# Re-ordering the last mixture-of-experts stage: first expert chunk behind the closing chunks, two smaller scan parts, gates in three groups, all read-backs at once

## The chip, the cores and the metric

The kernel runs on one core of a Trainium2 chip. The metric is device time in microseconds from the first to the last instruction of that core; lower is better. The engines are PE (matrix multiply), PEld (its weight loads), DVE (VectorE), ACT (ScalarE), POOL (GpSimd, which here issues all indirect gathers and scatters) and SP (which issues the plain DMAs).

## The reference, cut to what matters

The model has two layers, each a graph part plus a token mixer followed by a mixture of experts. The change touches only the last mixture of experts, `_L1_ffn_ref`, whose router is itself a small graph attention over 32768 edges between the first 2048 rows (B = 16, N = 128 in the source shapes; here it is called with one batch of 3125 rows):

```python
h = (x_flat @ W_gat).reshape(M, HEADS, NUM_EXPERTS)          # 4 heads, 4 experts
a_src = (h * att_src).sum(-1); a_dst = (h * att_dst).sum(-1)
e = leaky_relu(a_src[src] + a_dst[dst], 0.2)                  # per edge, loops added
alpha = exp(e - segment_max(e, dst)[dst]) / segment_sum(...)
agg = segment_sum(h[src] * alpha, dst) + b_gat
scores = layernorm(agg).reshape(M, HEADS, NUM_EXPERTS).mean(1)
topk_s, topk_i = top_k(scores, 2); w = softmax(topk_s)
for ei in range(4):
    g = where(topk_i == ei, w, 0).sum(-1)
    out = out + g * (gelu(x @ W1[ei] + b1[ei]) @ W2[ei] + b2[ei])
```

The expert outputs are computed for every row, the gates are needed only at the end: the matrix products of the experts and the per-edge work of the router can run side by side.

## The kernel before

The 3125 rows are 25 tiles of 125 rows (`P = 125`, `NT = 25`), grouped in seven chunks, `CHUNKS` (L22): four of 4 tiles and three of 3 tiles. The last stage is `layer1_ffn` (L1654). It goes through these steps.

**Closing chunks.** `close_graph` (L1906) finishes the layer before and feeds this stage. It runs a three-deep pipeline over chunks, steps c = 0 to 8: `in_units(c + 2)` scales on ACT, `moments(c)` adds to `x` and takes mean and variance on DVE, `rows(c - 1)` normalises on DVE, transposes on PE (L1951) and copies to `xT` on ACT (L1952), and `scores(c - 2)` multiplies by the router's weights on PE (L191), copies the result to `srow` and `row` on ACT (L1960, L1961) and stores `srow` to the table `tabg` in HBM. A dictionary `beside` names a step behind which a function is called; before, step `len(CHUNKS) - 3`, that is c = 4, calls the first expert's first chunk, `expert(0, *CHUNKS[0], *w)`. PE, DVE and ACT take all of this in the order in which it is written (`manual_schedule`, L1726).

**Scatters.** POOL scatters the 25 tiles of `row` to the table `starts` (line 58 as seen by the trace), tile by tile as `row` becomes ready.

**Gathers.** Each of the 256 edge columns (`EC = 256`, 128 edges each) needs one indirect gather of `tabg` rows into the tile `G` (`sources`, L1686; line 51 in the trace). They wait for all of `tabg`.

**Experts.** `expert` (L1704) runs 4 experts over 7 chunks: hidden products on PE into `fph` (L1709), GELU on ACT (L1711), second product on PE into `fpy` (L1717), bias add on DVE (L1719). Experts 0 and 1 stay in SBUF (`y`, `acc`), experts 2 and 3 are stored to HBM (`yd`). In this loop only DVE is held to the written order (L1801).

**Scans.** `scan(f0, f1)` (L1772) turns edge columns f0 to f1 into running segment sums: DVE adds and a running maximum (L1777 to L1784), two exponentials on ACT (L1786, L1792), a product (L1789) and 20 running sums (L1796), then a DMA of those columns of `G` to `sums` in HBM (L1797). `parts` (L1800) says behind which expert chunk (counted 1 to 28) which columns are scanned: the last part, columns 194 to 255, comes behind chunk 28.

**Carry and gates.** A short chain (L1820 to L1856) makes the carry between partitions, `taken`. POOL then gathers `g_r`, one row of `sums` per tile, 25 gathers. The outputs of experts 2 and 3 are loaded back as `yback`, four chunks at once and the others as one of five buffers is free (L1862 on). `graph_gates` (L1977) computes the gates for a group of tiles: DVE arithmetic, two exponentials, a square root (L2033), `top_two` (L625) in blocks of 5 tiles, another exponential, a normalisation. Two groups are used, chunks 0 to 3 (16 tiles) and chunks 4 to 6 (9 tiles).

**Totals.** For each tile the four expert outputs times their gates are added to `x`: even tiles of a chunk by four DVE instructions (L1892), odd tiles by four diagonal matrices from ACT (L1900), five PE products (L1898, L1902) and an ACT copy (L1903). A chunk is then stored to the output.

In this last part no engine is held to the written order; the program's planner may move instructions of one group between those of another.

Of the kernel before, what the change touches and what calls it, by code (L numbers as in the profile page):

```python
# [18 lines left out]
D = 256  # L19
P = 125  # L20
NT = 25
CHUNKS = ((0, 4), (4, 4), (8, 4), (12, 4), (16, 3), (19, 3), (22, 3))  # L22
# [20 lines left out]
E2, EC = 32768, 256  # L43
# [31 lines left out]
def rows_of(table):  # L75
    return table.rearrange("(t p) d -> p t d", p=P)
# [12 lines left out]
class Kernel:  # L89
# [532 lines left out]
                                     pattern=[[1, ne], [-1, ne]], channel_multiplier=0)  # L622
        return tie

    def top_two(self, pool, v, ne, tag, tie):  # L625

        nc, n = self.nc, v.shape[1]
        mask = pool.tile([P, n, ne], F32, name="mask" + tag)
        rank = pool.tile([P, n, ne], F32, name="rank" + tag)
        for t0 in range(0, n, 5):  # L630
            m = min(5, n - t0)
            s = slice(t0, t0 + m)
            shape = [P, m, ne, ne]
            gt = pool.tile([P, 5, ne, ne], F32, name="gt" + tag)[:, :m]
            eq = pool.tile([P, 5, ne, ne], F32, name="eq" + tag)[:, :m]
# [1018 lines left out]
    def layer1_ffn(self):  # L1654
        nc, tc, a = self.nc, self.tc, self.a
        NE, FC = 4, 4
        R = 24
        C = 25
        with ExitStack() as c:
            big = c.enter_context(tc.tile_pool(name="f1", bufs=1))  # L1660
            ps_a = c.enter_context(tc.tile_pool(name="f1pa", bufs=2, space=PSUM))
            ps_h = c.enter_context(tc.tile_pool(name="f1ph", bufs=3, space=PSUM))
# [41 lines left out]
            def expert(ei, t0, n, w1, w2, b2):  # L1704
                hs = wk.tile([128, FC, 4 * P], F32, name="fh")
                for f in range(FC):
                    ph = ps_h.tile([128, 4 * P], F32, name="fph")
                    for k in range(2):
                        nc.tensor.matmul(ph[:, :n * P], w1[:, k, f * 128:(f + 1) * 128],  # L1709
                                         xT[:, k, t0 * P:(t0 + n) * P], start=(k == 0), stop=(k == 1))  # L1710
                    nc.scalar.activation(hs[:, f, :n * P], ph[:, :n * P], AF.Gelu,  # L1711
                                         bias=self.col("L1_ffn_b1", ei * FC + f))
                out = y[ei][:, t0:t0 + n, :] if ei < 2 else wk.tile([P, 4, D], F32, name="fy")
                for i in range(n):
                    py = ps_y.tile([P, D], F32, name="fpy")
                    for f in range(FC):
                        nc.tensor.matmul(py, hs[:, f, i * P:(i + 1) * P], w2[:, f, :],  # L1717
                                         start=(f == 0), stop=(f == FC - 1))
                    nc.vector.tensor_add(out[:, i, :], py, b2)  # L1719
                if ei >= 2:  # L1720
                    move(nc.sync, rows_of(yd[ei - 2])[:, t0:t0 + n, :], out[:, :n, :])

            E_ = mybir.EngineType
            w = weights(0)
            with tc.tile_pool(name="f1l", bufs=1, side="right") as lp, \
                    tc.manual_schedule(engines={E_.PE, E_.DVE, E_.Activation}):  # L1726
                nc.vector.memset(row, 1.0)
                self.close_graph(lp, ps_a, ps_y, xT, acc, den, srow, row, tabg,
                                 beside={len(CHUNKS) - 3: lambda: expert(0, *CHUNKS[0], *w)})

                nc.vector.tensor_add(loop, srow[:, :, 16:20], row[:, :, 0:4])
                nc.vector.scalar_tensor_tensor(loop, loop, 0.2, loop, op0=OP.mult, op1=OP.max)
# [64 lines left out]
                nc.sync.dma_start(sums[:].rearrange("(p f) c -> p f c", p=128)[:, s, :], G[:, s, :])  # L1797


            parts = {10: (0, 80), 16: (80, 138), 22: (138, 194), 28: (194, EC)}  # L1800
            with tc.manual_schedule(engines={mybir.EngineType.DVE}):  # L1801
                step = -(-EC // (NE * len(CHUNKS)))
                sources(3 * step)
# [58 lines left out]
            rs = ga.tile([P, NT, R], F32, name="g_r", bufs=1)  # L1862
            backs = []
            for t0, n in CHUNKS:
                back = ga.tile([P, 2, 4, D], F32, name="yback", bufs=5)
                for i in range(2):
                    move(nc.sync, back[:, i, :n, :], rows_of(yd[i])[:, t0:t0 + n, :])
                backs.append(back)
                if len(backs) == 4:
                    break  # L1870
            for t in range(NT):
                gather(nc, rs[:, t, :], sums[:], self.seg_at[:, 1, t:t + 1])
            for c0, c1 in ((0, 4), (4, 7)):
                ta, tb = CHUNKS[c0][0], CHUNKS[c1 - 1][0] + CHUNKS[c1 - 1][1]
                more = ps_a.tile([P, 16, C], F32, name="ln_pt")
                for t in range(ta, tb):
                    nc.tensor.matmul(more[:, t - ta, :], ends[:, t * P:(t + 1) * P], taken, start=True, stop=True)
                gate = self.graph_gates(ga, ta, tb, rs, more[:, :tb - ta, :], loop, srow, vec, tie)
                for k in range(c0, c1):
                    t0, n = CHUNKS[k]  # L1880
                    if k < len(backs):
                        back = backs[k]
                    else:
                        back = ga.tile([P, 2, 4, D], F32, name="yback", bufs=5)
                        for i in range(2):
                            move(nc.sync, back[:, i, :n, :], rows_of(yd[i])[:, t0:t0 + n, :])
                    for t in range(t0, t0 + n):
                        outs = [y[ei][:, t, :] if ei < 2 else back[:, ei - 2, t - t0, :] for ei in range(NE)]
                        xs = self.x[:, t, :]
                        if (t - t0) % 2 == 0:  # L1890
                            for ei in range(NE):
                                nc.vector.scalar_tensor_tensor(xs, outs[ei], gate[:, t - ta, ei:ei + 1], xs,  # L1892
                                                               op0=OP.mult, op1=OP.add)
                            continue

                        diag = ga.tile([P, NE, P], F32, name="diag", bufs=3)
                        pm = ps_h.tile([128, 4 * P], F32, name="fph")[:P, :D]
                        nc.tensor.matmul(pm, self.ident[:P, :P], xs, start=True, stop=False)  # L1898
                        for ei in range(NE):
                            nc.scalar.activation(diag[:, ei, :], self.ident[:P, :P], AF.Copy,  # L1900
                                                 scale=gate[:, t - ta, ei:ei + 1])
                            nc.tensor.matmul(pm, diag[:, ei, :], outs[ei], start=False, stop=(ei == NE - 1))  # L1902
                        nc.scalar.copy(xs, pm)  # L1903
                    move(nc.sync, rows_of(self.out)[:, t0:t0 + n, :], self.x[:, t0:t0 + n, :])

    def close_graph(self, pool, psum, psum_g, xT, acc, den, srow, row, tabg, beside):  # L1906

# [69 lines left out]
    def graph_gates(self, ga, ta, tb, rs, more, loop, srow, vec, tie):  # L1977


        nc = self.nc  # L1980
        NE, n, s = 4, tb - ta, slice(ta, tb)
        r, loop = rs[:, s, :], loop[:, s, :]
# [15 lines left out]
        nc.vector.tensor_scalar(c2[:, :, 0, :], c2[:, :, 0, :], 0.0, None, op0=OP.min)  # L1998
        nc.vector.tensor_sub(c2[:, :, 1, :], loop, m)
        nc.scalar.activation(c2, c2, AF.Exp)  # L2000
        nc.vector.tensor_mul(c2[:, :, 0, :], c2[:, :, 0, :], hasb)
        agg = ga.tile([P, n, 16], F32, name="agg", bufs=1)
        own = ga.tile([P, n, 16], F32, name="g_own", bufs=1)
# [27 lines left out]
        nc.vector.tensor_mul(sq, agg, agg)  # L2031
        nc.vector.tensor_reduce(mu, sq, AX.X, OP.add)
        nc.scalar.activation(mu, mu, AF.Sqrt, bias=self.eps[:P], scale=1.0 / 16)  # L2033
        nc.vector.reciprocal(mu, mu)
        nc.vector.tensor_mul(agg, agg, mu[:, :, None].to_broadcast([P, n, 16]))
        nc.vector.tensor_mul(agg, agg, all_tiles(vec["ln_gamma"]))
# [1 line left out]
        sc = ga.tile([P, n, NE], F32, name="s_sc", bufs=1)  # L2038
        nc.vector.tensor_reduce(sc, agg.rearrange("p t (h e) -> p t e h", h=4), AX.X, OP.add)
        nc.vector.tensor_scalar(sc, sc, 0.25, None, op0=OP.mult)  # L2040
        mask = self.top_two(ga, sc, NE, "s", tie)
        gate = self.softmax_parts(ga, sc, NE, "s")
        nc.vector.tensor_mul(gate, gate, mask)
        self.normalise(ga, gate, NE, "s")
        return gate


@with_exitstack
# [42 lines left out]
```

## Time and profile before

| | us |
|---|---|
| runs (median of 3; lowest to highest) | 3070.16 (3053.29 to 3075.47) |
| the profiled execution, whole | 2708.31 |
| its span, first to last instruction | 2706.6 |
| PE busy | 2183.3 (81%) |
| POOL busy | 1661.2 (61%) |
| DVE busy | 1494.8 (55%) |
| ACT busy | 561.0 (21%) |

The profiled execution is 361.85 us shorter than the median of the runs; nothing in the profile says why. Times below are microseconds from the start of its span. In the last stage the following stretches can be told apart:

| stretch | us from the start | what runs |
|---|---|---|
| closing chunks with the first expert chunk among them | 2190 to 2254 | DVE, PE, ACT; POOL scatters from 2210.93 |
| expert loop | 2254 to 2592 | PE; POOL gathers `G` 2264.43 to 2595.5 |
| last scan and carry | 2597 to 2613 | DVE |
| gathers of `g_r` | 2614.93 to 2654.6 | POOL; loads of `yback` |
| gates and totals | 2641.6 to 2706.6 | DVE, ACT, PE |

A line of the timeline gives the start, the duration, the engine, the source line, the operation, output and input, the number of instructions that were merged, and in brackets the idle time of that engine just before and what ended it.

### The profile page before, as it was taken

Reading aid. Unit: us, or ns where it says so; the run is one execution under the profiler, and the core shown is the slowest. Engines: PE = TensorE matmul, PEld = TensorE weight load, DVE = VectorE, ACT = ScalarE, POOL = GpSimd, SP = SyncE. Lnnn points to the kernel's source line nnn. Section 1 sums busy time; section 2 is a strip of 40 time slices with the busy share of each in tenths; the row PEclk is TensorE's granted clock in tenths of the full one; section 3 lists DMA queues with packets and bytes.
Section 4 is the critical chain, followed back from the end, with each engine's and each line's share of the span. In section 5 each row is a group of like instructions: output and inputs, shape, how many; then the busy total and the mean of one; then the engine's idle time right before and its main releaser. Section 6 shows DMA issues by size and latency. Waiting matters only on the chain. (4 is left out here: it accounts for less than half of the span.)

```text
span 2706.6 us, 26634 instructions
## 1 busy us (share of the span) xinstructions
PE 2183.3 (81%) x9047; PEld 1643.4 (61%) x9047; DVE 1494.8 (55%) x3520; ACT 561.0 (21%) x1180; POOL 1661.2 (61%) x1486
## 2 busy tenths in 40 slices
PE   1852459999985999799999759999877779989953
PEld 1541347866754566588888646666655557666643
DVE  7977399465477931122122268998877762222226
ACT  1421000000001211122222244444100043132213
POOL 4888787776000731666666437778877726777751
PEclk9956669999995999899999879999899769999966
DMA  8930524043400212454555451111111121112252
GB/s 298 383 126 14 120 70 117 4 114 93 117 25 9 65 45 71 143 197 170 194 197 176 121 144 47 49 48 46 47 48 49 49 66 17 26 48 53 55 106 73
DMA packets 176141, 259.81 MB, mean 96 GB/s; under 512 B 54041, under 2 KB 141059, under 8 KB 172604
## 3 DMA queue, kind: packets, MB, share of 16 engines
q1 hardware_dynamic: 117803, 201.64, 24.0%
q0 software_dynamic: 52288, 47.17, 7.5%
q10 hardware_dynamic: 5894, 9.09, 1.0%
q8 instruction: 76, 1.25, 0.2%
q14 instruction: 80, 0.66, 0.1%
HBM read 173.99 MB, written 83.69 MB: 95 GB/s over the span
## 5 line engine op out<-in xcount | busy, mean ns | idle before, releaser
L58 POOL DMA_INDIRECT adj<-ch_sum,ch_place x391 | 508.3, 1300 | 149.9 <-issue 113.1
L51 POOL DMA_INDIRECT g<-tab,t_src x391 | 457.1, 1169 | 119.4 <-issue 108.7
L58 POOL DMA_INDIRECT sorted<-s_rows,pos x256 | 245.1, 958 | 182.0 <-DVE s_rows L1059 112.5
L460 PE MATMUL psum<-sup,adjT 125*125 125x256 f32 x1250 | 292.3, 393 | 52.7 <-DMA adjT<-adj 42.5
L1293 PE MATMUL pw<-v,hot 128*125 128x260 f32 x1244 | 306.9, 407 | 0.0
L51 POOL DMA_INDIRECT G<-tabg,g_src x256 | 253.4, 990 | 78.0 <-issue 71.3
L460 PEld LDWEIGHTS psum<-sup,adjT 125*125 125x125 f32 x1250 | 240.7, 194 | 94.1 <-DMA adjT<-adj 34.6
L1293 PEld LDWEIGHTS pw<-v,hot 128*125 128x125 f32 x1244 | 244.5, 200 | 43.6
L866 PE MATMUL ph<-xs,w 128*128 128x256 f32 x960 | 220.4, 389 | 23.6 <-issue 20.8
L866 PEld LDWEIGHTS ph<-xs,w 128*128 128x128 f32 x960 | 184.2, 194 | 59.0 <-issue 33.9
L894 PE MATMUL py<-w,h 128*128 128x256 f32 x960 | 216.7, 379 | 0.0
L894 PEld LDWEIGHTS py<-w,h 128*128 128x128 f32 x960 | 180.1, 190 | 23.3
L1717 PE MATMUL fpy<-fw,fh 128*125 128x256 f32 x800 | 181.4, 383 | 14.4 <-ACT fh L1711 11.7
L868 ACT ACTIVATE h<-ph,b 128x256 f32<-128x256 f32 x240 | 113.7, 474 | 363.0 <-PE ph L866 331.3
L1717 PEld LDWEIGHTS fpy<-fw,fh 128*125 128x125 f32 x800 | 150.3, 189 | 50.0 <-ACT fh L1711 15.0
L1709 PE MATMUL fph<-xT,fw 128*128 128x500 f32 (+1 forms) x448 | 177.2, 545 | 0.0
L1034 PE MATMUL pctx<-s_mv,s_ro 128*128 128x256 f32 x512 | 155.2, 414 | 1.9 <-DVE s_mv L1033 1.9
L58 POOL DMA_INDIRECT slots<-rows,abi x50 | 74.2, 1484 | 100.0 <-DVE r_cum L948 85.1
L897 DVE TENSOR_SCALAR yo<-py,own 128x256 f32<-128x256 f32 x60 | 27.8, 480 | 192.2 <-PE py L894 192.2
L463 DVE TENSOR_TENSOR x<-x,psum 125x512 f32<-125x512 f32 (+1 forms) x104 | 68.7, 663 | 108.8 <-PE psum L460 108.6
L1709 PEld LDWEIGHTS fph<-xT,fw 128*128 128x128 f32 x448 | 85.2, 192 | 71.4 <-issue 48.8
L170 ACT ACTIVATE ln_rs<-ln_mv,eps 125x4 f32<-125x4 f32 (+1 forms) x14 | 3.7, 294 | 586.6 <-DVE ln_mv L169 586.6
(550 smaller groups left out, 3423.9 us busy)
## 6 DMA issues: line engine op xcount, KB each, us to landing
adjT<-adj SPq DMA_DIRECT2D x25, 1367.2 KB
adj<-zero SPq DMA_DIRECT2D x22, 1536.0 KB
w<-in_L_ffn_W1p_dram SPq DMA_DIRECT2D x30, 1024.0 KB
w<-in_L_ffn_W2p_dram SPq DMA_DIRECT2D x30, 1024.0 KB
slots<-empty SPq DMA_DIRECT2D x1, 8448.0 KB
srow<-slots SPq DMA_DIRECT2D x30, 264.0 KB
adj<-ch_sum,ch_place POOLq DMA_INDIRECT x391
g<-tab,t_src POOLq DMA_INDIRECT x391
```

The costliest lines, as they stand in the source:

```text
L51: nc.gpsimd.indirect_dma_start(out=out, out_offset=None, in_=table, in_offset=bass.IndirectOffsetOnAxis(ap=idx, axis=0))
L58: return nc.gpsimd.indirect_dma_start(out=table, out_offset=bass.IndirectOffsetOnAxis(ap=idx, axis=0), in_=rows, in_offset=None, **kw)
L460: nc.tensor.matmul(pm[:, i, :], mats[b][:, (a0 + i) * P:(a0 + i + 1) * P], sup[:, b, :], start=(b == b0), stop=(b == b0 + n - 1))
L463: nc.vector.tensor_add(xs, xs, pm[:, :m, :])
L866: nc.tensor.matmul(ph, w1[:, k, f * 128:(f + 1) * 128], xs[:, k, :], start=(k == 0), stop=(k == 1))
L868: nc.scalar.activation(h[:, f, :], ph, AF.Gelu, bias=b1[:, f:f + 1])
L894: nc.tensor.matmul(py, h[:, f, i * 128:(i + 1) * 128], w2[:, f, :], start=(f == 0), stop=(f == FC - 1))
L897: nc.vector.tensor_scalar(yo, py, own[:, i, 2:3], None, op0=OP.mult)
L1034: nc.tensor.matmul(p1, ro[:, f - f0, :], mv, **st)
L1293: nc.tensor.matmul(pw.rearrange("p h c -> p (h c)"), hot[:, i - i0, :], v[:, i, :, :].rearrange("p h c -> p (h c)"), start=(i == i0), stop ...
L1709: nc.tensor.matmul(ph[:, :n * P], w1[:, k, f * 128:(f + 1) * 128], xT[:, k, t0 * P:(t0 + n) * P], start=(k == 0), stop=(k == 1))
L1717: nc.tensor.matmul(py, hs[:, f, i * P:(i + 1) * P], w2[:, f, :], start=(f == 0), stop=(f == FC - 1))
```

## The change

Five edits, all in the last stage.

- The first expert's first chunk is called behind step `len(CHUNKS) + 1`, the last step of the closing pipeline, and no longer behind c = 4.
- The last scan part (194 to 255) becomes two, 194 to 231 behind chunk 25 and 232 to 255 behind chunk 27, so that the last part stands before chunk 28 in DVE's order.
- All seven chunks of `yback` have a buffer of their own and are loaded before the gates.
- The gates are computed for three groups (chunks 0 and 1, 2 and 3, 4 to 6). `graph_gates` becomes a generator with three stops before it hands over the gate; at the first two stops of a group the totals of one waiting chunk of the group before are written in between. `top_two` takes blocks of 9 tiles there, and the softmax exponential is written ahead of it.
- PE, DVE and ACT are held to the written order in this part too.

```diff
-    def top_two(self, pool, v, ne, tag, tie):
+    def top_two(self, pool, v, ne, tag, tie, by=5):
...
-        for t0 in range(0, n, 5):
-            m = min(5, n - t0)
+        for t0 in range(0, n, by):
+            m = min(by, n - t0)
...
-                                 beside={len(CHUNKS) - 3: lambda: expert(0, *CHUNKS[0], *w)})
+                                 beside={len(CHUNKS) + 1: lambda: expert(0, *CHUNKS[0], *w)})
...
-            parts = {10: (0, 80), 16: (80, 138), 22: (138, 194), 28: (194, EC)}
+            parts = {10: (0, 80), 16: (80, 138), 22: (138, 194), 25: (194, 232), 27: (232, EC)}
...
-                back = ga.tile([P, 2, 4, D], F32, name="yback", bufs=5)
+                back = ga.tile([P, 2, 4, D], F32, name="yback", bufs=len(CHUNKS))
...
-                if len(backs) == 4:
-                    break
...
-            for c0, c1 in ((0, 4), (4, 7)):
+            def gates(c0, c1):
                 ta, tb = CHUNKS[c0][0], CHUNKS[c1 - 1][0] + CHUNKS[c1 - 1][1]
                 more = ps_a.tile([P, 16, C], F32, name="ln_pt")
                 for t in range(ta, tb):
                     nc.tensor.matmul(more[:, t - ta, :], ends[:, t * P:(t + 1) * P], taken, start=True, stop=True)
-                gate = self.graph_gates(ga, ta, tb, rs, more[:, :tb - ta, :], loop, srow, vec, tie)
+                for gate in self.graph_gates(ga, ta, tb, rs, more[:, :tb - ta, :], loop, srow, vec, tie):
+                    yield gate, ta
+            def total(k, gate, ta):
...
+            with tc.manual_schedule(engines={E_.PE, E_.DVE, E_.Activation}):
+                ready = []
+                for c0, c1 in ((0, 2), (2, 4), (4, 7)):
+                    for gate in gates(c0, c1):
+                        if gate[0] is None and ready:
+                            total(*ready.pop(0))
+                    while ready:
+                        total(*ready.pop(0))
+                    ready = [(k, *gate) for k in range(c0, c1)]
+                for r in ready:
+                    total(*r)
...
         nc.scalar.activation(c2, c2, AF.Exp)
+        yield None
         nc.vector.tensor_mul(c2[:, :, 0, :], c2[:, :, 0, :], hasb)
...
         nc.scalar.activation(mu, mu, AF.Sqrt, bias=self.eps[:P], scale=1.0 / 16)
+        yield None
...
-        mask = self.top_two(ga, sc, NE, "s", tie)
         gate = self.softmax_parts(ga, sc, NE, "s")
+        yield None
+        mask = self.top_two(ga, sc, NE, "s", tie, 9)
...
-        return gate
+        yield gate
```

`total` holds the lines of the loop over a chunk's tiles (L1887 to L1905) unchanged, and reads `backs[k]`.

More of the change, by code (lines that the diff above doesn't have):

```diff
@@ L629, in top_two @@
         rank = pool.tile([P, n, ne], F32, name="rank" + tag)
-        for t0 in range(0, n, 5):
-            m = min(5, n - t0)
+        for t0 in range(0, n, by):
+            m = min(by, n - t0)
             s = slice(t0, t0 + m)
             shape = [P, m, ne, ne]
-            gt = pool.tile([P, 5, ne, ne], F32, name="gt" + tag)[:, :m]
-            eq = pool.tile([P, 5, ne, ne], F32, name="eq" + tag)[:, :m]
+            gt = pool.tile([P, by, ne, ne], F32, name="gt" + tag)[:, :m]
+            eq = pool.tile([P, by, ne, ne], F32, name="eq" + tag)[:, :m]
             other = v[:, s, None, :].to_broadcast(shape)
@@ L1877, in layer1_ffn @@
                     nc.tensor.matmul(more[:, t - ta, :], ends[:, t * P:(t + 1) * P], taken, start=True, stop=True)
-                gate = self.graph_gates(ga, ta, tb, rs, more[:, :tb - ta, :], loop, srow, vec, tie)
[L1879 to L1898, printed above, removed]
-                        for ei in range(NE):
[L1900 to L1904, printed above, removed]
@@ new lines, in gates @@
+                for gate in self.graph_gates(ga, ta, tb, rs, more[:, :tb - ta, :], loop, srow, vec, tie):
+                    yield gate, ta
+            def total(k, gate, ta):
+                t0, n = CHUNKS[k]
+                for t in range(t0, t0 + n):
+                    outs = [y[ei][:, t, :] if ei < 2 else backs[k][:, ei - 2, t - t0, :] for ei in range(NE)]
+                    xs = self.x[:, t, :]
+                    if (t - t0) % 2 == 0:
+                        for ei in range(NE):
+                            nc.vector.scalar_tensor_tensor(xs, outs[ei], gate[:, t - ta, ei:ei + 1], xs,
+                                                           op0=OP.mult, op1=OP.add)
+                        continue
+                    diag = ga.tile([P, NE, P], F32, name="diag", bufs=3)
+                    pm = ps_h.tile([128, 4 * P], F32, name="fph")[:P, :D]
+                    nc.tensor.matmul(pm, self.ident[:P, :P], xs, start=True, stop=False)
+                    for ei in range(NE):
+                        nc.scalar.activation(diag[:, ei, :], self.ident[:P, :P], AF.Copy,
+                                             scale=gate[:, t - ta, ei:ei + 1])
+                        nc.tensor.matmul(pm, diag[:, ei, :], outs[ei], start=False, stop=(ei == NE - 1))
+                    nc.scalar.copy(xs, pm)
+                move(nc.sync, rows_of(self.out)[:, t0:t0 + n, :], self.x[:, t0:t0 + n, :])
```

## The prediction

> **What bounds the kernel now.** I read first the chain of waits, for what ends last; its last links are the whole end of the kernel (start, duration, piece):
>
> ```profile
> 2594.58 2.21 DMA G<-tabg,g_src
> ...
> 2605.02 5.70 DVE G L1796 x20
> 2610.78 3.16 DMA sums<-G
> ...
> 2614.93 1.22 POOL g_r L51
> ...
> 2651.13 3.45 DMA g_r<-sums,g_ati
> ...
> 2697.12 3.51 DMA yback<-yd
> ```
>
> The last gather of `G` releases the last scan, that releases a store, that releases 25 gathers of `g_r`, then come the gates and totals, and even a load of `yback`. So I went to the timeline of POOL in front of that gather:
>
> ```profile
> 2227.32 1.18 POOL L58 DMA_INDIRECT starts<-row,g_ati  x1 [0.30 <-issue]
> 2245.02 1.24 POOL L58 DMA_INDIRECT starts<-row,g_ati  x1 [16.52 <-ACT row L1961]
> ...
> 2264.43 0.99 POOL L51 DMA_INDIRECT G<-tabg,g_src  x1 [0.30 <-issue]
> ...
> 2380.31 4.23 POOL L51 DMA_INDIRECT G<-tabg,g_src  x1 [0.31 <-issue]
> ```
>
> Scatters and gathers run back to back (0.30 us apart) but for one hole of 16.52 us, in which POOL waits for `row` of chunk 3. Who suffers later is in the timeline of all engines:
>
> ```profile
> 2367.84 0.95 DVE L1777 TENSOR_TENSOR g_e<-g_e,G 128x320 f32<-128x320 f32 x1 [8.45 <-DMA G<-tabg,g_src]
> 2375.96 5.30 PE L1717 MATMUL fpy<-fw,fh 128*125 128x256 f32 x16 [9.97 <-ACT fh L1711]
> ...
> 2597.18 0.77 DVE L1777 TENSOR_TENSOR g_e<-g_e,G 128x248 f32<-128x248 f32 x1 [4.98 <-DMA G<-tabg,g_src]
> ...
> 2641.63 0.23 DVE L1985 TENSOR_TENSOR g_m<-g_r,loop 125x64 f32<-125x64 f32 x1 [17.65 <-DMA g_r<-sums,g_ati]
> 2655.25 0.20 DVE L1985 TENSOR_TENSOR g_m<-g_r,loop 125x36 f32<-125x36 f32 x1 [8.69 <-DMA g_r<-sums,g_ati]
> ```
>
> The first scan waits 8.45 us for gathers, and PE behind it 9.97 us; the last waits 4.98 us although PE ended at 2591.4: gathers lead, PE follows within 5 us. In the end part DVE idles 17.65 and 8.69 us for `g_r`.
>
> **Part 1, first expert chunk behind the closing chunks.** Before, PE, ACT and DVE leave the closing chunks at 2220.3 for 16 products L1709 (9.57 us) and 32 of L1717 (7.07), and come back at 2237.16 (DVE's `moments(5)`). Without it DVE would go on at 2215.9; chunks 4 to 6 took it 4.2 us each (2237.16 to 2241.3 and so on). PE is as tight. Its row for 16 products L191 is 3.48 us up to 2220 and 1.82 at 2242, when the expert has warmed the clock:
>
> ```profile
> 2210.00:2228.00 18.00, 18.00 (x62) 13.19 (x62) 5.66 (x20) 9.60 (x31) 13.70 (x12) 0.57 0.15 10
> 2228.00:2245.00 17.00, 17.00 (x73) 11.68 (x72) 9.18 (x33) 6.87 (x12) 0.50 (x1) 1.00 0.01 0
> ```
>
> (columns: stretch, length, busy PE, PEld, DVE, ACT, POOL, granted clock, DMA share, GB/s). The Trainium skill, "TensorE: Matmul & The Clock Gate", Part 1, says the full clock comes after some 3.4 us of sustained activity. By that rule the closing chunks, busy since 2206.6, would be fast without the expert; the trace had 0.57, so I take the slow rows: 16 + 16 products and three sets of 12 (2.6 each) and transposes of 1.5 put `row` of chunk 3 at 2225.7 and of chunk 6 at 2236.7 (by the rule some 5 us earlier). POOL needs them at 2228.5 and 2243.3 (12 and 22 scatters of 1.487 from 2210.93), so both answers close the hole: scatters end at 2248.1, gathers start 16.3 us earlier, the last lands at 2596.8 - 16.3 = 2580.5.
>
> With the chunk go 4 GELUs and a table load on ACT and 4 adds (0.42) on DVE, which now stand behind the closing chunks; it issues no DMA, and SP's stores of `tabg` for chunks 3 to 6 no longer follow it (chunk 6's, about 2240, is ahead of the gathers' 2248).
>
> PE pays: chunk 0 starts at 2236.5 and takes 16.1 (2220.3 to 2236.4). Before, PE had done chunk 0 by 2236.4 and, between the last closing chunks, another 22 products of L1709 (9.2 us) by 2253.7; now it has chunk 0 alone by 2252.6: 8.1 us behind. But the first scan, at chunk 10, finds its 80 columns at 2351 and no longer waits. PE's loss there was 12.8 us (chunk 11's L1717 due at 2377.5, seen at 2390.3) against 2.6 at the scan of chunk 22 (due 2537.8, seen 2540.4): 10.2 us back. PE's end moves by -2.1.
>
> **Part 2, two small scans.** The scan behind chunk 25 adds 2.6 to PE: PE ends at 2591.9, chunk 27 (10.2 earlier, the row spacing of 3-tile chunks) at 2581.7. It now runs beside gathers, and this case has a price for it: in each earlier part one gather took 4.23, 4.06 and 3.70 us instead of 0.94 and came free 0.8 us behind the 20 scans L1796. The skill speaks for nothing here: "SBUF — State Buffer", Who interferes with whom, has a DVE instruction with two SBUF inputs contend only with GpSimd's reads, and infers that descriptor writing needs the write interface, so a scan would cost a gather nothing. The rows win: +3.0 (by the rule 0). Last gather 2583.5, DVE starts 0.4 later at 2583.9: gathers and PE end within 2 us of each other.
>
> The last scan has 24 columns instead of 62. Its 20 scans do not shrink in the rows (5.43, 5.55, 5.46, 5.69 us for 80, 58, 56, 62), so I keep 5.0; L1777 to L1791 shrink from about 5 to 2.6; but beside chunk 28 the exponentials swap tables with GELU, and DVE waits 2.46 + 1.87 there (row of chunk 22) instead of 0.76. Sum 11.5 us against 13.6. Bounds 9 (table swaps hidden) and 14 (as now). DVE's adds for chunk 28, its store, and the carry (2.3 us behind the scan now) queue behind the scan; their cover is the 14 us until gates can start. PE does not stop for the delayed adds: chunk 28 has 3 tiles and `fpy` 3 buffers. Store to first gather stays 4.15 (2610.78 to 2614.93). So `g_r` starts at 2583.9 + 11.5 + 4.15 = 2599.6 against 2614.93: -15.3.
>
> **Part 3, gates and totals.** Call the start of `g_r` T. Before, the last DVE instruction ends at T + 86.7 and the span at T + 91.7. Eight gathers at 1.505 us and 4.1 from issue to DVE (2637.54 to 2641.63) free the first group at T + 14.7; the second is there at T + 26.7, the third at T + 40.2. A group costs DVE, from the 9-tile rows at their spacing (0.23 for 36 elements, 0.34 for 144): 11 instructions 2.4; 19 with two reciprocals, 5.3; 8 to the softmax, 2.3; `top_two` in one block (15 instructions over all groups for 30 now) and the rest, 2.5: 12.5. Three groups for two is one group more. The first, with nothing to hide its exponential and root, costs 14.2. Totals are 14 tiles x 4 at 0.40 = 22.4, unchanged. Written order: 14.7 + 14.2 + 12.5 + 12.5 + 22.4 = T + 76.3, and 4.8 to the end as now: T + 81.1. Gain 10.6. Two more table loads for the root and two for the exponential (1.28 each) lie on ACT between totals; a chunk costs ACT at most 4.6 (two odd tiles at 2.3), DVE has 5.3 + 3.2 there. If ACT's cover fails, each of four stops costs up to 3 us.
>
> **Part 4, all loads at once.** 28 DMAs on SP (0.3 us issue each), 6.4 MB, 34 us at the 189 GB/s of 2615 to 2642: done by T + 37, chunk 6 needed at T + 72. The 2.90 us wait in front of the last DVE instruction is in Part 3's gain. SP's order puts them behind the store of chunk 28; `g_r` is POOL's and passes them. That gathers land late beside loads: landing was the same beside them (4.09) and after them (4.12), so 0; bound +10.
>
> **Sum.** 15.3 + 10.6 = 26 off the profiled 2708.3: 2682, ratio 0.9904. The median of the runs is 361.85 us longer, and no view says where. Subtracted as it is the sum gives 3044, by the ratio 3041; I take 3042.
>
> **Rivals.**
> *PE binds in the runs.* If the extra 362 us are PE's, the experts end well behind the gathers, the first scan never waited, and Part 1 costs its 8.1 and Part 2 its 2.6; Chunk 27 ends 10.2 before PE's end and the scan takes 11.5, so `g_r` follows PE's end by 1.3 + 4.15 and no longer by 0.4 + 13.6 + 4.15, 12.7 gained for 10.7 paid; with Part 3's 10.6 that is -12.6, 3058. For: PE is 81% busy. Against: the profile has it at 0.98 clock in this stretch.
> *More than the sum.* If the stage stretches with POOL in the runs (its hole too), and the swaps hide: -36, 3034.
> *Slower: loads starve the small gathers.* Place: T to T + 64. The loads kept 0.99 of DMA time; at 100 GB/s (the page's slices of this part have 106 and 73) 6.4 MB take 64 us. If `g_r` rows land only behind them, gates start at T + 64 and end at T + 64 + 62 + 4.8 = T + 131: 39 lost, 15 gained, +24, 3094; at 73 GB/s (88 us) +48, 3118. It decides once rows land later than T + 41. Against: the two landings above.
> *It does nothing:* if the planner had hidden the hole elsewhere; the hole is on record, so small.
>
> **Chances.** The sum 0.62 (3042, own range 3028 to 3056), more 0.17, PE 0.11, slower and unforeseen order effects 0.10. A measurement of this kernel tells about 1% from no change, so the bound is 3039.5: 0.28 of the first case and all of the second lie below, 0.45; above 3100.9 0.10 with the tail of the last; 0.45 between. The range 3016 to 3066 leaves out the slower case and the tails.
>
> **What would show it.** POOL's hole gone and the first gather at 2248; no wait at the first L1777; last scan ending near 2595 with `g_r` at 2600; DVE busy without holes over 1 us from T + 15; span end at T + 81. It is wrong if chunk 0 starts later than 2245, if a `G` gather waits, or if ACT holds DVE in the totals.

## The result and the profile after

| | us |
|---|---|
| before, median of 17 runs (lowest to highest) | 3070.16 (3053.29 to 3086.59) |
| after, median of 17 runs (lowest to highest) | 3051.88 (3035.7 to 3113.44) |
| ratio, with its 95% interval | 0.992 [0.9897, 0.9943] |
| span of the profiled execution of after | 3053.0 |

The changed kernel is faster by 18 us in the medians of all runs and by 25 us by the ratio. The ratio compares only runs in the faster of two states in which one kernel can run; 5 of the 17 runs of after were in the slower one. The forecast was 3042 us, 28 us below before, from a sum of 26 us off the profile.

The profile that the forecast was read from had a span of 2706.6 us. In the runs below the time of before went with the chip: on two chips all its runs took between 3058 and 3157 us, on a third all took between 2700 and 2711. It was compared with its variants on both kinds; each ratio below is against runs of before on the same chip and occasion. A second profile of before, taken where it takes 3080 us, gives the missing side. Measured from the first instruction of the closing chunks, with T for the first gather of `g_r`:

| us from the start of the closing chunks | before, span 2706.6 | before, span 3076.5 | after, span 3053.0 |
|---|---|---|---|
| first gather of `G` | 74.7 | 73.4 | 58.6 |
| last gather of `G` issued | 404.8 | 478.7 | 471.8 |
| last expert add (DVE) | 402.0 | 528.7 | 525.6 |
| last scan starts | 407.4 | 529.1 | 513.5 |
| T | 425.2 | 546.9 | 530.0 |
| gates start, behind T | 26.7 | 26.6 | 19.6 |
| T to the end | 91.7 | 92.6 | 90.2 |
| whole stage | 516.8 | 639.5 | 620.2 |

Against the second profile of before the stage is 19.3 us shorter: 16.9 up to T, 2.4 behind it. The remaining few us of the spans' difference of 23.5 lie ahead of the stage, where nothing was changed. One profile is one execution: the kernel with both alterations, further down, has the same expert loop, its last expert add at 532.4 and T at 536.5, so the 16.9 is not exact to some 7 us.

The list of waits of after says what fills the long execution (engine, what waited, what ended it: us in total, times, longest):

```profile
DVE x L463 <- remote: 136.9, 5, 40.5
...
ACT fh L1711 <- remote: 88.0, 10, 42.1
POOL G L51 <- DVE g_src L1691: 87.5, 15, 16.5
...
DVE y L1719 <- remote: 21.3, 2, 18.5
```

"Remote" means that no event of this core's trace ended the wait. (Below, such a wait is called a stop.) The first profile of before has no such wait at all, and none of POOL for `g_src` in the gathers of `G`. Two of these rows, `fh` and `y`, lie in the expert loop. There the order of the first profile is turned round: gathers of `G` are issued 41.7 us before the last scan needs them, POOL waits for indices from the expert loop's DVE, and the experts end last.

POOL's timeline of after answers the hole of 16.52 us:

```profile
2453.99 1.23 POOL L58 DMA_INDIRECT starts<-row,g_ati  x1 [20.54 <-ACT row L1971]
...
2489.92 1.18 POOL L58 DMA_INDIRECT starts<-row,g_ati  x1 [0.30 <-issue]
...
2491.42 1.00 POOL L51 DMA_INDIRECT G<-tabg,g_src  x1 [0.16 <-issue]
```

All 25 scatters follow each other without a hole, some 1.5 us apart, and the first gather comes 58.6 us behind the start of the closing chunks; the forecast put it at 58.2 (2248 less 2189.8). The end part, in the timeline of all engines of after:

```profile
2946.28 0.40 DVE L1777 TENSOR_TENSOR g_e<-g_e,G 128x96 f32<-128x96 f32 x1
...
2953.48 3.83 DVE L1796 TENSOR_TENSOR_SCAN G<-g_e,G 128x24 f32<-128x24 f32 x20 [2.46 <-ACT g_e L1792]
...
2957.38 0.34 SPq L1797 DMA_DIRECT2D sums<-G  x1
...
2962.82 1.22 POOL L51 DMA_INDIRECT g_r<-sums,g_ati  x1 [57.30 <-issue]
...
2982.37 0.19 DVE L1996 TENSOR_TENSOR g_m<-g_r,loop 125x32 f32<-125x32 f32 x1 [20.60 <-DMA yback<-yd]
...
2997.39 0.48 DVE L1889 SCALAR_TENSOR_TENSOR x<-y,sm_exs,x 125x256 f32<-125x256 f32 x1
2997.90 0.48 DVE L1889 SCALAR_TENSOR_TENSOR x<-acc,sm_exs,x 125x256 f32<-125x256 f32 x1
2998.42 1.01 DVE L1889 SCALAR_TENSOR_TENSOR x<-yback,sm_exs,x 125x256 f32<-125x256 f32 x2
```

The last scan no longer waits for a gather, is 11.0 us long (2946.28 to 2957.31), and `g_r` follows its store by 5.4 us. Then comes the part that went wrong: gates start 19.6 us behind T, not 14.7, and the four sums of a tile stand 0.51 us apart, not 0.40.

### The profile page after: what moved, and what is told of

It reads as the page before. It is cut to its first block, busy times and chain, and to the rows that moved or that the text cites. A ratio compares the mean times of both kernels' runs of the same rounds, so it can differ in the third digit from the quotient of the medians.

```text
span 3053.0 us, 26728 instructions
## 1 busy us (share of the span) xinstructions
PE 2260.7 (74%) x9047; PEld 1671.3 (55%) x9047; DVE 1511.2 (49%) x3578; ACT 570.1 (19%) x1193; POOL 1635.4 (54%) x1486
## 3 DMA queue, kind: packets, MB, share of 16 engines
q8 instruction: 76, 1.25, 0.2%
## 5 line engine op out<-in xcount | busy, mean ns | idle before, releaser
L58 POOL DMA_INDIRECT adj<-ch_sum,ch_place x391 | 484.3, 1239 | 149.9 <-issue 121.0
L51 POOL DMA_INDIRECT g<-tab,t_src x391 | 456.7, 1168 | 119.4 <-issue 110.2
L460 PE MATMUL psum<-sup,adjT 125*125 125x256 f32 x1250 | 326.8, 410 | 221.8 <-issue 180.6
L460 PEld LDWEIGHTS psum<-sup,adjT 125*125 125x125 f32 x1250 | 249.5, 202 | 288.4 <-issue 199.3
L866 PE MATMUL ph<-xs,w 128*128 128x256 f32 x960 | 220.5, 388 | 45.7 <-issue 38.9
L1717 PE MATMUL fpy<-fw,fh 128*125 128x256 f32 x800 | 202.8, 409 | 58.9 <-ACT fh L1711 29.1
L463 DVE TENSOR_TENSOR x<-x,psum 125x512 f32<-125x512 f32 (+1 forms) x104 | 68.8, 664 | 332.7 <-remote 136.9
L1717 PEld LDWEIGHTS fpy<-fw,fh 128*125 128x125 f32 x800 | 159.8, 203 | 108.1 <-issue 43.7
L1711 ACT ACTIVATE fh<-fph,cols 128x500 f32<-128x500 f32 (+1 forms) x112 | 69.8, 632 | 366.9 <-PE fph L1709 237.5
```

Of the source, the lines that this page charges most:

```text
L51: nc.gpsimd.indirect_dma_start(out=out, out_offset=None, in_=table, in_offset=bass.IndirectOffsetOnAxis(ap=idx, axis=0))
L58: return nc.gpsimd.indirect_dma_start(out=table, out_offset=bass.IndirectOffsetOnAxis(ap=idx, axis=0), in_=rows, in_offset=None, **kw)
L460: nc.tensor.matmul(pm[:, i, :], mats[b][:, (a0 + i) * P:(a0 + i + 1) * P], sup[:, b, :], start=(b == b0), stop=(b == b0 + n - 1))
L463: nc.vector.tensor_add(xs, xs, pm[:, :m, :])
L866: nc.tensor.matmul(ph, w1[:, k, f * 128:(f + 1) * 128], xs[:, k, :], start=(k == 0), stop=(k == 1))
```

## The experiments

### Each part alone

Four kernels on one chip, where before took 3080.96 us (median of 51 runs). The first is the kernel before, profiled again.

> The kernel before, unchanged, for a second profile. Gathers-bind theory (as in the first profile of before, 2706.6 us): no stops without a releaser, last G gather ends 3 to 5 us behind PE, span near 2707. Experts-bind theory (the changed kernel's profile has 333 us of stops on ACT and DVE that nothing in the trace ends): span near 3068, such stops of some 300 us here too, POOL waits for the copies of g_src in the expert loop, and the last G gather ends some 50 us before PE does. T to the end of the span near 91.7 us in both (T: start of the first g_r gather).

3078.22 us, span 3076.5. Its list of waits has what the first profile had not:

```profile
DVE x L463 <- remote: 185.7, 6, 41.4
...
ACT fh L1711 <- remote: 108.0, 9, 74.9
...
POOL G L51 <- DVE g_src L1691: 80.5, 15, 14.8
```

So the long executions are the kernel's, not the change's, and in them the experts bind: the last scan, written behind the last chunk, starts 0.4 us behind the last expert add (529.1 and 528.7), and 50 us behind the last gather. The next three kernels are the kernel before with one part of the change each.

```diff
-                                 beside={len(CHUNKS) - 3: lambda: expert(0, *CHUNKS[0], *w)})
+                                 beside={len(CHUNKS) + 1: lambda: expert(0, *CHUNKS[0], *w)})
```

> Only the first edit (first expert chunk behind the closing chunks). Gathers-bind theory: the hole of 16.5 us on POOL goes, T comes 7.5 us earlier, ratio 0.9975. Experts-bind theory: the hole goes too but gathers were not late; PE loses the overlap of 8 us with the last closing chunks, ratio 1.000 to 1.003.

3065.79 us, ratio 0.9964 [0.9947, 0.9981]. The first gather comes at 58.5 us behind the start of the closing chunks (73.4 before), the last expert add at 520.6 (528.7), T at 538.7 (546.9). This is the surprise of the study: PE was to pay for the moved chunk, the experts bind, and yet they end 8.1 us earlier. The gain is sure from the ratio, 6 to 16 us; its size in single profiles is less so, as said above.

```diff
-            parts = {10: (0, 80), 16: (80, 138), 22: (138, 194), 28: (194, EC)}
+            parts = {10: (0, 80), 16: (80, 138), 22: (138, 194), 25: (194, 232), 27: (232, EC)}
```

> Only the second edit (columns 194 to 231 scanned behind chunk 25, 232 to 255 behind chunk 27). Gathers-bind theory: the last scan still waits for the last gather, T moves by -1 to +2 us, ratio 1.000. Experts-bind theory: the scan moves beside chunk 28, T comes 10 us earlier (12.7 less 2.6), ratio 0.9967 or less.

3071.8 us, ratio 0.997 [0.9947, 0.9993]. The last expert add is 5.3 us later (534.0), but T follows it by 4.2 us (538.2) and no longer by 18.2, since the scan stands before the last adds. Net 8.7 us. The timeline of this kernel shows it:

```profile
2955.47 3.83 DVE L1796 TENSOR_TENSOR_SCAN G<-g_e,G 128x24 f32<-128x24 f32 x20 [2.46 <-ACT g_e L1792]
...
2959.41 0.40 DVE L1719 TENSOR_TENSOR fy<-fpy,fb 125x256 f32<-125x256 f32 x1
...
2960.07 0.72 DVE L1719 TENSOR_TENSOR fy<-fpy,fb 125x256 f32<-125x256 f32 x2
...
2964.55 1.22 POOL L51 DMA_INDIRECT g_r<-sums,g_ati  x1 [57.05 <-DVE g_taken L1855]
```

The three last adds now queue behind the scan and run under the store of `sums`; what releases `g_r` is DVE's carry and no longer that store.

The third takes the rest: gates in three groups, all loads at once, the written order in the end part.

```diff
-                back = ga.tile([P, 2, 4, D], F32, name="yback", bufs=5)
+                back = ga.tile([P, 2, 4, D], F32, name="yback", bufs=len(CHUNKS))
...
-            for c0, c1 in ((0, 4), (4, 7)):
+            with tc.manual_schedule(engines={E_.PE, E_.DVE, E_.Activation}):
+                ready = []
+                for c0, c1 in ((0, 2), (2, 4), (4, 7)):
```

> Only the last part (three groups of gates in written order, all loads at once). By the prediction's sum: T to the end 81 us, 10.6 us gained, ratio 0.9965. By the changed kernel's profile (T to the end 90.2 us): 1.5 us gained, ratio 0.9995; DVE starts the gates near T + 19.5.

3072.32 us, ratio 0.9999 [0.998, 1.0018]: nothing that can be told from no change. From T to the end 90.2 us against 92.6. Taken by their ratios the three parts are worth 11, 9 and 0 us; the whole change 25 in the first measurement and 18 in a second one (below). In the profiles T comes 8.1 us earlier by the first part, 8.7 by the second and 16.9 by the whole change. The forecast had given the end part 10.6.

### The end part taken apart

Two alterations of the changed kernel, on a chip where before took 2703.61 us (median of 11 runs). In the first, the four sums of a chunk's two even tiles alternate in DVE's order.

```diff
-                for t in range(t0, t0 + n):
...
+                for ei in range(NE):
+                    for t in range(t0, t0 + n, 2):
+                        xs = self.x[:, t, :]
+                        nc.vector.scalar_tensor_tensor(xs, outs_of(t)[ei], gate[:, t - ta, ei:ei + 1], xs,
+                                                       op0=OP.mult, op1=OP.add)
+                for t in range(t0 + 1, t0 + n, 2):
...
-                    if (t - t0) % 2 == 0:
-                        for ei in range(NE):
-                            nc.vector.scalar_tensor_tensor(xs, outs[ei], gate[:, t - ta, ei:ei + 1], xs,
-                                                           op0=OP.mult, op1=OP.add)
-                        continue
```

> The changed kernel with the DVE totals of a chunk's two even tiles alternating, so that an instruction does not follow the one whose result it adds to. If the 0.51 us spacing of the changed profile (0.40 before, where the planner had paired them) comes from that dependence: spacing 0.40, 7 chunks x 8 x 0.11 = 6 us less, T to the end 84 us. If it is the written order as such or memory traffic: 90 us.

2686.1 us, ratio 0.9927 [0.9911, 0.9944]; T to the end 86.3 us, where 84 were expected. The changed kernel's own end part was measured on this chip in the few-ahead variant further down, which differs from it ahead of T alone: 89.0. The timeline of the sums in the alternating kernel:

```profile
2632.94 0.87 DVE L1890 SCALAR_TENSOR_TENSOR x<-y,sm_exs,x 125x256 f32<-125x256 f32 x2
2633.73 0.87 DVE L1890 SCALAR_TENSOR_TENSOR x<-acc,sm_exs,x 125x256 f32<-125x256 f32 x2
2634.52 1.66 DVE L1890 SCALAR_TENSOR_TENSOR x<-yback,sm_exs,x 125x256 f32<-125x256 f32 x4
2636.10 0.18 DVE L2015 TENSOR_TENSOR g_c<-g_c,g_has 125x32 f32<-125x32 f32 x1
```

Eight sums in 3.16 us, 0.395 each; in the changed kernel the same eight take 3.91 (2997.39 to 3001.30, one small instruction behind), 0.49 each. The first profile of before had them alternating too, because the planner was free to place them:

```profile
2669.28 0.87 DVE L1892 SCALAR_TENSOR_TENSOR x<-y,sm_exs,x 125x256 f32<-125x256 f32 x2
2670.07 0.88 DVE L1892 SCALAR_TENSOR_TENSOR x<-acc,sm_exs,x 125x256 f32<-125x256 f32 x2
2670.86 1.67 DVE L1892 SCALAR_TENSOR_TENSOR x<-yback,sm_exs,x 125x256 f32<-125x256 f32 x4
```

In the second, `yback` has two buffers, and the load of chunk k + 2 is written behind the totals of chunk k.

```diff
-            for t0, n in CHUNKS:
-                back = ga.tile([P, 2, 4, D], F32, name="yback", bufs=len(CHUNKS))
+            def load_back():
+                if len(backs) == len(CHUNKS):
+                    return
+                t0, n = CHUNKS[len(backs)]
+                back = ga.tile([P, 2, 4, D], F32, name="yback", bufs=2)
...
+            for _ in range(2):
+                load_back()
...
                 move(nc.sync, rows_of(self.out)[:, t0:t0 + n, :], self.x[:, t0:t0 + n, :])
+                load_back()
```

> The changed kernel with two buffers of yback: loads of two chunks at T, the others each behind the totals of the chunk two before. If loads of all chunks at once delay the small gathers of g_r: DVE starts the gates at T + 14.7 and not at T + 19.5, 5 us less to the end, unless a later load is waited for. If the delay comes from elsewhere (three groups, buffers freed late): still T + 19.5, and T to the end 90 us or more.

2682.07 us, ratio 0.9917 [0.9901, 0.9932]; gates start 13.5 us behind T and T to the end is 84.6. The first instruction of the gates in this kernel:

```profile
2609.28 0.26 DVE L2003 TENSOR_TENSOR g_m<-g_r,loop 125x32 f32<-125x32 f32 x1 [14.33 <-DMA g_r<-sums,g_ati]
```

and in the few-ahead variant on the same chip, which loads all at once:

```profile
2620.16 0.19 DVE L1996 TENSOR_TENSOR g_m<-g_r,loop 125x32 f32<-125x32 f32 x1 [20.06 <-DMA yback<-yd]
```

The eight gathers are issued at the same pace in both. With all loads in flight DVE begins 19.0 us behind T, with two chunks of loads 13.5. The second line names a load as the releaser, but the instruction reads `g_r` and `loop`, not `yback`: it waits for several semaphores, and the name is that of the event nearest in time. What it lacked was the eighth gather. In the trace of after this gather is issued 10.6 us behind T and its last completion comes at 19.0; with two chunks of loads it comes at 13.2. The medians from issue to landing of all 25 gathers say the same, with all loads at once (the alternating kernel) and with two chunks (this one):

```profile
g_r<-sums,g_ati POOLq DMA_INDIRECT x25, 7.3
```

```profile
g_r<-sums,g_ati POOLq DMA_INDIRECT x25, 3.4
```

### Both alterations

> The changed kernel with both alterations of its end part: loads of yback two chunks ahead only, and the sums of a chunk's even tiles interleaved on DVE. If the late start of the gates (4.9 us late) and the spacing of dependent sums (0.51 for 0.40) are two separate terms, the gains add: from the first g_r gather to the end 82 us (88.9 less 4.4 less 2.6), 6 to 7 us less than the changed kernel, a ratio some 0.0025 below it. Rival, both are cover for the same wait (ACT's diagonals or the last load): 84 to 85 us, no better than the loads alone.

On a chip where before took 3085.02 us (median of 32 runs): 3057.84 us, ratio 0.9933 [0.9906, 0.996]; the changed kernel itself, beside it:

> The changed kernel itself, beside two variants of its end part. On a chip on which the kernel before takes about 2704 us: ratio 0.994 (g_r at 410 us from the start of the closing chunks, 89 us from there to the end). On one on which it takes about 3070 us: 0.992 to 0.994, with one stop of 40 us or more on ACT in the expert loop.

3064.0 us, ratio 0.9941 [0.9921, 0.9961]. The ratios are 0.0008 apart where 0.0025 was expected, and their intervals overlap; the traces part the end parts: gates start 13.6 us behind T, and T to the end is 82.4 us, against 90.2 in the profile of after and 89.7 on this chip in the one-step-ahead kernel of the next section, which has the end part of after. That is 7.3 us for 7.1 as the sum of the two alone, so in the end part the two terms add. The rival, that both hide under one wait, had 84 to 85. That the whole kernel is faster by it is not shown.

### How far ahead the indices are handed out

The long stops on ACT, PE and DVE in the expert loop end near the moment at which POOL runs out of indices. In the second profile of before POOL ran out at 148.2 and ACT's stop of 74.92 us ended at 163.2, counted from the start of the closing chunks; with the first part of the change alone 120.8 and 114.8 (a stop of 46.23). That suggests a cause, and a cheap test of it: `sources(n)` has DVE copy the next n columns of indices, and POOL can issue no more gathers than that.

```diff
-                sources(3 * step)
+                sources(step)
```

This is the few-ahead variant, one step of 10 columns; a second kernel has `sources(6 * step)`. Both were run twice. On the chip with before at 2703.61 us:

> The changed kernel with 10 gathers of G handed to POOL ahead of the expert loop and not 30 (each expert chunk still hands out 10). Theory that the long stops of ACT, PE and DVE last as long as POOL has gathers to issue: POOL runs out 20 gathers (25 us) sooner, the long ACT stop (42 us in the changed kernel's profile) shrinks to about 20, PE ends some 20 us earlier, ratio 0.985. Theory that the stops belong to fixed places of ACT's, DVE's and PE's own instruction streams: same stop, ratio 0.992. Gathers-bind theory: gathers later, ratio above 0.993.

> The changed kernel with 60 gathers handed to POOL ahead of the expert loop and not 30: the suspected cost doubled. Stops-last-while-POOL-gathers theory: 30 gathers (37 us) more in one run, the long ACT stop grows by about 37 us, ratio near 1.004. Fixed-places theory: ratio 0.992. Gathers-bind theory: no later than 0.992, as gathers are never held back.

2688.13 us, ratio 0.9938 [0.9924, 0.9952], and 2686.04 us, ratio 0.9939 [0.992, 0.9958]. There is no stop in either trace and nothing to tell apart, so this says nothing of the cause. It says what the change does where gathers bind: T at 411.1 and 409.5 us (425.2 before), T to the end 89.0 and 88.9. Here, where the sum of the forecast belongs, the change is worth 15 to 18 us of the 26. On the chip with before at 3085.02 us:

> Indices of G handed to POOL one step ahead instead of three. Theory A, that the stops of ACT and PE in the expert loop last as long as POOL has gathers to issue: where the kernel before takes about 3070 us the first stop ends earlier (near 80 us from the start of the closing chunks for 111) and is shorter than 25 us; total within 10 us of the changed kernel. Theory B, that the stops don't depend on POOL: a stop of 40 us stays. Where it takes about 2704 us there are no stops, and nothing changes (0.994).

> Indices of G handed to POOL six steps ahead instead of three. Theory A: where the kernel before takes about 3070 us the first stop ends when POOL runs out, some 60 to 90 us later than in the changed kernel, and the kernel is longer by 15 us or more. Theory B: a stop of some 42 us as before, and the same time within 5 us. Where it takes about 2704 us nothing changes (0.994).

3042.36 us (4 runs), ratio 0.9867 [0.9816, 0.9919], and 3093.74 us (20 runs), ratio 1.0023 [1.0005, 1.0042]: 0.7% below and 0.8% above the changed kernel. One line decides which of them is faster than before. One step ahead, in the timelines of ACT and POOL:

```profile
2529.09 1.81 ACT L1711 ACTIVATE fh<-fph,cols 128x500 f32<-128x500 f32 x3 [18.80 <-remote]
2529.74 0.94 POOL L51 DMA_INDIRECT G<-tabg,g_src  x1 [4.42 <-DVE g_src L1691]
```

Three steps ahead, the changed kernel, with PE's timeline:

```profile
2507.42 5.19 PE L1709 MATMUL fph<-xT,fw 128*128 128x500 f32 x12
...
2543.45 0.68 ACT L1711 ACTIVATE fh<-fph,cols 128x500 f32<-128x500 f32 x1 [42.06 <-remote]
2544.18 2.04 PE L1709 MATMUL fph<-xT,fw 128*128 128x500 f32 x2 [31.57 <-issue]
...
2570.06 0.95 POOL L51 DMA_INDIRECT G<-tabg,g_src  x1 [16.47 <-DVE g_src L1691]
```

Six steps ahead, with DVE's:

```profile
2564.75 0.68 ACT L1711 ACTIVATE fh<-fph,cols 128x500 f32<-128x500 f32 x1 [51.05 <-remote]
2575.89 0.68 ACT L1711 ACTIVATE fh<-fph,cols 128x500 f32<-128x500 f32 x1 [10.46 <-remote]
...
2615.09 0.42 DVE L1719 TENSOR_TENSOR y<-fpy,fb 125x256 f32<-125x256 f32 x1 [61.10 <-remote]
2620.16 0.94 POOL L51 DMA_INDIRECT G<-tabg,g_src  x1 [16.25 <-DVE g_src L1691]
```

POOL's wait in brackets gives the moment at which it ran dry (start of the line less its idle time). Counted from the start of the closing chunks:

| steps ahead | one | three (after) | six |
|---|---|---|---|
| gathers issued before POOL runs dry | 20 | 50 | 80 |
| POOL runs dry | 83.5 | 120.8 | 158.5 |
| last add of the third expert chunk | 102.1 | 136.5 | 174.0 |
| stops of ACT at `fh`, in all | 69.7 | 88.0 | 140.7 |
| whole stage | 592.6 | 620.2 | 650.1 |

Without stops the third chunk's last add starts at 88.1 (the one-step kernel on the other chip). With them it comes 15.5 to 18.6 us behind the moment at which POOL runs dry, and moves with it: by 34.4 and 37.5 us for 30 gathers more, which take 37.5 at 1.25 each. Theory B, stops that don't depend on POOL, is out. Theory A is right in the large and not in each stop: the six-step kernel is over 15 us longer than the changed one, as it said, and the one-step kernel's first stop ends at 87.2 (near 80 expected) and is 18.8 us long (under 25). But the one-step kernel gained more than the 10 us it allowed, and the six-step kernel's first stop on ACT is 51.05 us and ends at 119.4, long before POOL runs dry; what grew there is the series behind it, one GELU per 11.2 us, and a stop of 61.1 us on DVE.

The stop itself is no wait for a result. In the changed kernel PE had ended the 12 products in front of ACT's GELU by 2512.6, and PE is the one other engine for which that GELU waits; ACT began it at 2543.45.

The few-ahead kernel is the fastest of all on this chip, from 4 runs. Its union with the two alterations of the end part wasn't run.

## Why the prediction came out as it did

**Up to T: the size was right, and its cause only where the first profile holds.** Predicted 15.3 us. Where gathers bind the variants have 13.9 to 15.7 (T at 409.5 to 411.3 against 425.2), and the steps are there one by one: first gather 58.5 us behind the start (predicted 58.2), last scan started at 394.2 in the few-ahead variant (394.1). Closing chunks, hole and stream were read rightly from the trace. Some of its terms were off by a us or so and made up for each other. No gather beside the scan behind chunk 25 took longer than 1.51 us, where I had added 3.0, though beside the three larger scans one again took 4.24, 4.07 and 3.70; here the answer of the Trainium skill, "SBUF — State Buffer", Who interferes with whom (no cost), was nearer than the rows of the larger scans. The 20 scans L1796, flat from 80 to 56 columns, do shrink below that: 5.43 us for 80, 4.51 for 38, 3.83 for 24 in the few-ahead variant, where I kept 5.0; so the last part took 11.0, not 11.5. Against that T follows the store by 5.4 us, not 4.15, because the chunk's own `yd` store and the carry now stand behind the scan.

**Where before takes 3070 us T came 16.9 us earlier, for other reasons.** The rival *PE binds in the runs* described them: experts end well behind the gathers, `g_r` follows PE's end. It had 12.7 us gained for 10.7 paid (8.1 and 2.6). The scans did what it says, with other sizes: 14.0 gained behind the last add, 5.3 paid for 2.6. Its other price, that the moved chunk costs PE 8.1 us, came out as a gain of 8.1. The rival took the extra 362 us for a slower PE; in the stage under change they are stops, and the moved chunk shortens those: POOL's gathers begin 15 us earlier and, since chunk 0 with its handing-out no longer precedes them, the first stretch holds 50 gathers for 60 ((148.2 - 73.4) / 1.25 and (120.8 - 58.5) / 1.25), so POOL runs dry 27 us earlier. That this is what made the 8.1 is argued from the few-ahead and more-ahead pair; it wasn't isolated further. So the forecast of the time is near in part by luck: the first edit helps in both worlds by two unrelated ways, and its 15.3 us met a gain of much the same size that the sum did not contain.

**The end part was mis-sized: 10.6 us predicted, 2.4 to 2.8 measured.** The working was 14.7 to the gates, 39.2 for three groups, 22.4 of totals, 4.8 to the end (the profile of before has 5.0 there): T + 81.1. The profile of after has 19.6, 38.9, 27.5 and 4.2: T + 90.2. The gates, the part with most working in it, are right within 0.3. Two terms failed; mended, they give back some 7 of the 8 us that were missing.

- *Totals unchanged at 0.40.* The row of 0.40 was of alternating tiles; held to the written order, each sum waits for the one before it. 56 of them at 0.49 are 5.1 us more. The alternating kernel takes 22.2 for them; of the 5 us 2.7 reach the end, among other things because DVE then waits longer for ACT's softmax exponential (1.67 and 1.50 us for 0.55 and 0.79 in the few-ahead variant).
- *All loads at once at 0.* I judged from two landings of single rows, 4.09 and 4.12 us, that loads don't delay the gathers. With all 28 loads in flight eight rows are in DVE's hands 19.0 to 20.1 us behind T, with eight loads at first 13.5. That is 5 us in the bound of 0 to 10 that the prediction gave. The first profile of before held it: there the eighth gather, issued 10.6 us behind T, has its last completion at 18.8. That cost nothing there, because the first group waited for the sixteenth. And the sixteenth, issued at 2637.54 and read as a landing beside the loads, came as the loads ended (columns as in the prediction, DMA share and GB/s last):

```profile
2632.00:2635.00 3.00, 0.00 (x0) 0.00 (x0) 0.00 (x0) 0.00 (x0) 2.39 (x3) 0.50 1.18 207
2637.50:2642.00 4.50, 0.00 (x0) 0.00 (x0) 0.33 (x2) 0.00 (x0) 3.60 (x3) 0.50 0.41 69
```

The rival *Slower* named this mechanism and this place; it needed rows later than T + 41 to decide the sign, and got T + 19.6.

With both mended the end part is T + 82.4, so the plan of the forecast was there to be had.

**The clock rule against the row** was decided for the row. The windows of the few-ahead variant (columns as in the prediction, granted clock third from the end), whose closing chunks are those of the changed kernel:

```profile
2210.00:2228.00 18.00, 18.00 (x88) 17.59 (x87) 15.79 (x54) 9.53 (x36) 13.44 (x12) 0.50 0.16 12
2228.00:2245.00 17.00, 17.00 (x57) 11.86 (x57) 0.06 (x1) 5.78 (x13) 13.65 (x12) 0.67 0.15 8
2245.00:2262.00 17.00, 17.00 (x66) 11.99 (x65) 2.98 (x8) 2.71 (x4) 13.16 (x15) 1.00 0.24 46
```

PE is busy for all of the first stretch at half the clock, and full clock comes only with the expert's products, which start at 2234.93 (predicted 2236.5). The closing products kept their slow durations, 3.48 us for 16 in the row of the weight loads, as taken. Activity of this kind, 18 us of it, didn't bring the full clock that the Trainium skill, "TensorE: Matmul & The Clock Gate", Part 1, gives after some 3.4. **ACT's cover** failed by 1.7 us in all (0.96 and 0.78 at L2057 in after), a little of what was allowed for.

## What to carry to other kernels

Before predicting from one profile, compare its span with the runs: here they were 362 us apart, and 123 us of the missing time lay in the stage under change and made another engine the one that ends last. When a planner's freedom is replaced by a written order, look at what it had interleaved: durations read from its rows include that. Read-backs that are needed late should not be put in flight beside small gathers that are needed at once.

## What the runs showed of the hardware that was not expected

- While POOL issued a stream of indirect gathers, ACT, PE and DVE stopped for 10 to 75 us at a time with nothing in this core's trace that ends the wait; how long the expert loop was held followed how many gathers POOL had to issue. The same code on another chip has no such stop. Why is open: whether issuing or moving the rows does it wasn't tried. The stops of an earlier stage that no kernel here altered (DVE at L463: 136.9 us in after) fall into such streams as well: of the 311 us of stops over 8 us in the profile of after, 279 lie where POOL issues indirect DMAs back to back, which is 2015 of the span's 3053 us. But the longest of these streams, 391 DMAs from 1837 to 2412 us, has no stop over 8 us in it, so a stream alone is not enough.
- A small indirect gather of `g_r` landed in 7.3 us (median) with 28 loads in flight and in 3.4 with eight at first.
- A DVE sum that depends on the one before it took its turn at 0.51 us, an independent one at 0.40 (125x256 elements).
- A gather beside 20 scans was held 4.24 us at 80 columns, at most 1.51 us at 38, against 0.94 alone (few-ahead variant).
